# The context's tails on 128 partitions, the last key added by VectorE, five small loads moved one tile of tokens later

## The chip, the cores and the metric

The kernel runs on one core of a Trainium2 chip. The metric is the device time of one execution in microseconds (us). Before the change, three runs took 673.49, 671.36 and 673.45 us; the median is 673.45.

## The reference

A small Perceiver layer in float32, in three blocks with residual sums: cross-attention to a context, linear attention with an MLP, and a mixture of experts. Only the first block is touched. There are 8 sequences of 64 tokens with 512 features (`x`), and each sequence attends to a context of its own of 1601 keys:

```python
def _L0_xattn_ref(proj_p, proj_q, W, b):
    trans_q = jnp.einsum('bqh,oh->bqo', proj_q, W) + b
    att_weights = jnp.einsum('bph,bqh->bpq', proj_p, trans_q)
    att_norm = jax.nn.softmax(att_weights, axis=-1)
    att_vec = jnp.einsum('bpq,bqh->bph', att_norm, proj_q)
    out = jax.nn.relu(jnp.einsum('bph,oh->bpo', att_vec, W) + b)
    return out
...
x = x + _L0_xattn_ref(_layernorm(x, axis=-1), ctx_1024, L0_xattn_W, L0_xattn_b)
```

`proj_p` is the normalized `x` (8, 64, 512), `proj_q` the context (8, 1601, 512). The context is read twice: once transposed for the scores, once by rows for the weighted sum.

## The kernel before, in words

**Tiles.** The 512 tokens are four tiles of 128 (`NT` = 4). A tile holds two sequences, 64 tokens each, in the two halves of the 128 partitions. For a tile `t` the work is:

- `key_group(t, g)`, g = 0 to 3 (L412): the scores against 401 or 398 keys, from the transposed context (`ctxT`); for each half a product of 128 rows by 64 columns. ScalarE brings them into the buffer `scores` with the bias `pb` (L431). After the fourth group `softmax` (L437) takes the maximum on VectorE and the exponential on ScalarE, with the row sums.
- `turn_scores(t)` (L445): TensorE transposes the exponentials in blocks of 128 keys (L456), and ScalarE copies them into `eT` (L457). The 1601 keys are three groups of 512 and a tail of 65 (`TAIL`). The tail's block is one transpose to 65 partitions (L459) and one copy (L460).
- `weigh(t, g)`, g = 0 to 2 (L464): the weighted sum of the context's rows (`ctx`) in one PSUM bank `av`, for each half a product of 128 keys by 64 columns (L472). After the third group the tail's product is added (L482), with 65 keys in the contraction, and VectorE scales the sum by the inverse row sum into `av_sb` (L490).
- `turn_av(t)` (L492, the transposes at L495, VectorE's copy at L497), `attended(t)` (L499, the product with W at L502), `add_and_normalize(t)` (L506), `turn_h(t)` (L514) and `values(t, n)` (L528, the product at L532), which belongs to the linear attention that follows.

TensorE carries out a float32 product as two passes, so the profile counts two instructions for each product; a transpose is one.

**Order.** `tc.manual_schedule` makes every engine and SP's queue follow the order in which the program is written out. The loop over tiles (L541 to L569) interleaves the groups of one tile with the key groups of the next ones: behind the third `weigh` of tile `t` come `key_group(t + 2, 0)`, `turn_av(t)`, `key_group(t + 2, 1)` and `attended(t)`; for the last two tiles `values(t - 2, 0)` and `values(t - 2, 1)` take the place of the key groups.

**Loads.** All large loads come from SP's queue in the order of a list (L133 to L167). They go to a ring of 12 buffers, of up to 1 MB each; a load can be written out when the load 12 places earlier is done with (`issue_to`, L175). For tile `t` the list has rows 0, keys 2 of the next tile, rows 1, keys 3 of the next tile, rows 2, the tail, then keys 0 and 1 of tile `t + 2`; every rows or keys entry is two loads, one for each sequence. Behind tile 2's tail stand the two halves of `wv`, and behind tile 3's tail `wq`, `wk`, `wo` and the weights of the MLP. The tails have two buffers of their own (L74) and are loaded by one DMA each, to partitions 0 to 64, with both sequences side by side (L188).

**late_loads.** This function (L402) issues five DMAs from SP: it writes zeros, taken from the part of `v_sb` for tile 3, to the spare rows of the output and to the table of the experts' tokens, and loads the bias `b2_bc` and, in two halves, `proj2`. It is called once, behind the third `weigh` of tile 1 (L557). `proj2` is first used by the linear attention (L611).

Of the kernel before, what the change touches and what calls it, by code (L numbers as in the profile page):

```python
# [17 lines left out]
ALU = mybir.AluOpType  # L18
AX = mybir.AxisListType

P = 128
B, S, D = 8, 64, 512
LK = 1601
NT = B * S // P
KC = D // P
GK = 512
NG = LK // GK
TAIL = LK - NG * GK
SW = -(-LK // 4)
WIDTHS = [min(SW, LK - SW * g) for g in range(4)]  # L30
H, DH = 16, 64
# [15 lines left out]
def perceiver_kernel(  # L47
# [22 lines left out]
    nc = tc.nc  # L70
# [11 lines left out]
    def mm_bank(name):  # L82
        return ps.tile([P, 512], F32, tag="mm", name=name)

    def acc_bank(name):
        return ps.tile([P, 512], F32, tag="acc", name=name)
# [85 lines left out]
    def in_ring(key):  # L172
        return key[0] not in places_of and key not in places_of and key[0] != "tail"

    def issue_to(n):  # L175

        while issued[0] < min(n, len(order)):
            key, src = order[issued[0]]
            if in_ring(key) and len(held) >= RING:
                if held[0] not in freed:  # L180
                    return
                held.pop(0)
            if key in places_of:
                t_ = places_of[key]
                nc.sync.dma_start(t_, src)
            elif key[0] == "tail":
                t_ = tails.tile([P, 2, D], F32, tag="tail", name="_".join(str(k) for k in key))
                nc.sync.dma_start(t_[:TAIL, :, :], src)  # L188
            else:
                width = WIDTHS[key[2]] if key[0] == "ctxT" else 512  # L190
                t_ = ring.tile([P, 4, width], F32, tag="ring", name="_".join(str(k) for k in key))
                nc.sync.dma_start(t_, src)
                held.append(key)
            streamed[key] = t_
            issued[0] += 1

    def done(*keys):

        freed.update(keys)

    def need(*key):
        if key[0] not in ("ctxT", "ctx", "tail", "wv"):
            done(*[k for k in held if place[k] < place[key] - AHEAD + 1])
            issue_to(place[key] + 1 + AHEAD)
        else:
            issue_to(len(order))
        return streamed[key]


    ident = const.tile([P, P], F32, name="ident")  # L210
# [153 lines left out]
    def pw_half(half, hc):  # L364
# [10 lines left out]
        nc.scalar.copy(pw_t[:, hc, cols], bank[:, : 2 * P])  # L375

    issue_to(len(order))
    turn_p(0)
    turn_p(1)
# [22 lines left out]
    def late_loads():  # L402
        nc.sync.dma_start(out[B * S :, :], zero[:, :D])
        nc.sync.dma_start(table.rearrange("p k two -> p (k two)"), zero[:, : NE * NI * 2])
        nc.sync.dma_start(b2_bc, b2.partition_broadcast(P))
        for r in range(2):
            nc.sync.dma_start(proj2[r * DH : (r + 1) * DH, :], proj)


    all_scores, all_rinv, all_et = {}, {}, {}  # L410

    def key_group(t, g):  # L412

        if t >= NT:
            return
        if g == 0:
            all_scores[t] = xa2.tile([P, LK], F32, tag="scores", name=f"scores_{t}")
        width = WIDTHS[g]
        sc = acc_bank(f"sc_{t}_{g}")
        keys = [need("ctxT", t, g, h) for h in range(2)]  # L420
        for c in range(KC):
            for h in range(2):
                nc.tensor.matmul(  # L423
                    sc[h * S : (h + 1) * S, :width],
                    pw_t[:, c, (2 * t + h) * S : (2 * t + h + 1) * S],
                    keys[h][:, c, :],
                    start=(c == 0),
                    stop=(c == KC - 1),
                )
        done(*[("ctxT", t, g, h) for h in range(2)])  # L430
        nc.scalar.activation(  # L431
            all_scores[t][:, g * SW : g * SW + width], sc[:, :width], AF.Identity, bias=pb[:, t : t + 1]
        )
        if g == 3:
            softmax(t)
# [9 lines left out]
    def turn_scores(t):  # L445
        scores = all_scores[t]
        rinv = small.tile([P, 1], F32, tag="rinv", name=f"rinv_{t}")
        nc.vector.reciprocal(rinv, all_rinv[t])
        all_rinv[t] = rinv
        e_t = all_et[t] = xa.tile([P, 4 * NG + 1, P], F32, tag="w", name=f"eT_{t}")  # L450
        for g in range(NG + 1):
            bank = mm_bank(f"et_{t}_{g}")
            if g < NG:
                for j in range(4):
                    k = g * GK + j * P
                    nc.tensor.transpose(bank[:, j * P : (j + 1) * P], scores[:, k : k + P], ident)  # L456
                nc.scalar.copy(e_t[:, 4 * g : 4 * g + 4, :].rearrange("p j q -> p (j q)"), bank)  # L457
            else:
                nc.tensor.transpose(bank[:TAIL, :P], scores[:, NG * GK : LK], ident)  # L459
                nc.scalar.copy(e_t[:TAIL, 4 * NG, :], bank[:TAIL, :P])  # L460

    all_av, all_xo = {}, {}

    def weigh(t, g):  # L464

        if g == 0:
            all_av[t] = acc_bank(f"av_{t}")
        av, e_t = all_av[t], all_et[t]
        rows = [need("ctx", t, g, h) for h in range(2)]
        for j in range(4):  # L470
            for h in range(2):
                nc.tensor.matmul(  # L472
                    av[h * S : (h + 1) * S, :],
                    e_t[:, 4 * g + j, h * S : (h + 1) * S],
                    rows[h][:, j, :],
                    start=(g == 0 and j == 0),
                    stop=False,
                )
        done(*[("ctx", t, g, h) for h in range(2)])
        if g == NG - 1:  # L480
            for h in range(2):
                nc.tensor.matmul(  # L482
                    av[h * S : (h + 1) * S, :],
                    e_t[:TAIL, 4 * NG, h * S : (h + 1) * S],
                    need("tail", t)[:TAIL, h, :],
                    start=False,
                    stop=True,
                )
            av_sb = all_av[t] = xa2.tile([P, D], F32, tag="tmp", name=f"av_sb_{t}")
            nc.vector.tensor_scalar(av_sb, av, all_rinv[t], None, ALU.mult)  # L490

    def turn_av(t):  # L492
        bank = mm_bank(f"avt_{t}")
# [12 lines left out]
    def add_and_normalize(t):  # L506
        o_sb = xa2.tile([P, D], F32, tag="tmp", name=f"o_sb_{t}")
        nc.vector.tensor_tensor(o_sb, all_xo[t], xb_bc, ALU.add)
        nc.vector.scalar_tensor_tensor(xs[:, t, :], o_sb, 0.0, xs[:, t, :], ALU.max, ALU.add)
        normalize(xin[:, t, :], xs[:, t, :], *statistics(xs[:, t, :], f"xin_{t}"), f"xin_{t}")  # L510
        hns[t] = xa2.tile([P, D], F32, tag="tmp", name=f"hn_{t}")
        normalize(hns[t], xin[:, t, :], *statistics(xin[:, t, :], f"h_{t}"), f"h_{t}")

    def turn_h(t):  # L514
        bank = mm_bank(f"tr_h_{t}")
        for c in range(KC):
            nc.tensor.transpose(bank[:, c * P : (c + 1) * P], hns[t][:, c * P : (c + 1) * P], ident)
        for c in range(KC):
            nc.vector.tensor_scalar(  # L519
                h_t[:, c, t * P : (t + 1) * P],  # L520
                bank[:, c * P : (c + 1) * P],
                g1_c[:, c : c + 1],
                beta1_c[:, c : c + 1],
                ALU.mult,
                ALU.add,
            )

    def values(t, n):  # L528
        wv_n = need("wv", n)
        bank = mm_bank(f"v_{n}_{t}")  # L530
        for c in range(KC):
            nc.tensor.matmul(  # L532
                bank, h_t[:, c, t * P : (t + 1) * P], wv_n[:, c, :], start=(c == 0), stop=(c == KC - 1)
            )
        nc.scalar.copy(v_sb[:, t, n * 512 : (n + 1) * 512], bank)
# [5 lines left out]
    for t in range(NT):  # L541
        turn_scores(t)
        if t == NT - 1:

            nc.scalar.activation(warm0, eps, AF.Sqrt)
        if t > 0:
            add_and_normalize(t - 1)
        weigh(t, 0)
        key_group(t + 1, 2)
        if 0 < t < NT - 1:  # L550
            turn_h(t - 1)
        weigh(t, 1)
        if t == NT - 1:
            turn_h(t - 1)
        key_group(t + 1, 3)
        weigh(t, 2)
        if t == NT - 3:  # L557
            late_loads()

        if t < NT - 2:  # L560
            key_group(t + 2, 0)
        else:
            values(t - 2, 0)
        turn_av(t)
        if t < NT - 2:
            key_group(t + 2, 1)
        else:
            values(t - 2, 1)
        attended(t)  # L569
# [411 lines left out]
    bank = mm_bank("counts")  # L981
# [446 lines left out]
```

## Time and profile before

| What | Value |
|---|---|
| Median of three runs | 673.45 us (671.36 to 673.49) |
| The profiled execution | 672.11 us, of which the span in the trace is 670.4 us |
| Mean granted TensorE clock | 0.981 |
| PE busy | 627.2 us (94%) |
| DVE, ACT, POOL busy | 175.5, 128.3, 61.6 us |
| DMA | 138.08 MB, mean 206 GB/s |
| PE L472, the weighted sum | 50.2 us busy, 7.3 us idle before it |
| PE L482, the tail's product | 6.8 us busy in 16 instructions |
| SP L188, the tail's load | 4 DMAs of 260 KB |

PE is TensorE's matmuls, PEld its weight loads, DVE is VectorE, ACT is ScalarE, POOL is GpSimd, SP is SyncE, whose queue (SPq) issues the loads. In the page's second part the span is cut into 40 equal slices, and each digit is a share in tenths. A line of the timeline has start, duration, engine, line of the kernel, operation, the tile written and the tiles read, and in brackets the idle time ahead and what ended it. A line of the windows has the busy time of each engine with its number of instructions, then the granted clock, the DMA engines' share and the GB/s moved. A group of instructions has the shapes, the number, the busy time, the mean duration in ns, and the idle time ahead of it.

### The profile page before, as it was taken

Reading aid. Unit: us, or ns where it says so; the run is one execution under the profiler, and the core shown is the slowest. Engines: PE = TensorE matmul, PEld = TensorE weight load, DVE = VectorE, ACT = ScalarE, POOL = GpSimd, SP = SyncE. Lnnn points to the kernel's source line nnn. Section 1 sums busy time; section 2 is a strip of 40 time slices with the busy share of each in tenths; the row PEclk is TensorE's granted clock in tenths of the full one; section 3 lists DMA queues with packets and bytes.
Section 4 is the critical chain, followed back from the end, with each engine's and each line's share of the span. In section 5 each row is a group of like instructions: output and inputs, shape, how many; then the busy total and the mean of one; then the engine's idle time right before and its main releaser. Section 6 shows DMA issues by size and latency. Waiting matters only on the chain. (4 is left out here: it accounts for less than half of the span.)

```text
span 670.4 us, 6808 instructions
## 1 busy us (share of the span) xinstructions
PE 627.2 (94%) x2664; PEld 291.2 (43%) x2664; DVE 175.5 (26%) x419; ACT 128.3 (19%) x240; POOL 61.6 (9%) x81
## 2 busy tenths in 40 slices
PE   4998989799999999999999998899999899999993
PEld 3743434243444444454444455433444344334441
DVE  4011323122316888650000045311210111100100
ACT  2241222220132223031011211211111211111110
POOL 2000000000000000060000001340202202210000
PEclk9998999899999999999999999799999999999997
DMA  8999999999421203030213115029389576694611
GB/s 326 420 420 389 420 384 418 374 386 413 194 111 43 85 1 127 1 126 18 107 64 125 63 64 188 3 69 350 137 314 337 176 314 229 205 359 177 269 16 19
DMA packets 24224, 138.08 MB, mean 206 GB/s; under 512 B 4164, under 2 KB 4164, under 8 KB 11896
## 3 DMA queue, kind: packets, MB, share of 16 engines
q1 hardware_dynamic: 20056, 129.90, 49.7%
q0 software_dynamic: 3024, 6.58, 4.4%
q10 hardware_dynamic: 1104, 1.07, 0.5%
q8 instruction: 25, 0.41, 0.2%
q14 instruction: 15, 0.12, 0.1%
HBM read 132.56 MB, written 4.97 MB: 205 GB/s over the span
## 5 line engine op out<-in xcount | busy, mean ns | idle before, releaser
L1097 PE MATMUL up<-e_up,xgT 128*128 128x512 f32 x224 | 100.2, 595 | 1.2 <-PEq L1326 1.2
L1097 PEld LDWEIGHTS up<-e_up,xgT 128*128 128x128 f32 x224 | 40.9, 190 | 50.4 <-issue 50.4
L1105 PE MATMUL y<-e_wo,hidT 128*128 128x512 f32 x128 | 61.0, 599 | 0.0
L808 PE MATMUL mlp<-w,hid_sb 128*128 128x512 f32 x128 | 58.8, 597 | 0.0
L1062 DVE TENSOR_TENSOR mid<-up,act 128x256 f32<-128x256 f32 x35 | 14.9, 425 | 162.4 <-ACT act L1060 162.4
L472 PE MATMUL av<-ctx,eT 128*64 128x512 f32 x192 | 50.2, 636 | 7.3 <-DMA ctx<-in_ctx_dram 6.5
L787 PE MATMUL hid<-v_sb,w 128*128 128x512 f32 (+2 forms) x144 | 56.6, 545 | 0.0
L423 PE MATMUL sc<-ctxT,pw_t 128*64 128x401 f32 (+1 forms) x256 | 48.1, 501 | 0.6 <-DMA ctxT<-in_ctx_T_dram 0.6
L787 PEld LDWEIGHTS hid<-v_sb,w 128*128 128x128 f32 x144 | 26.2, 190 | 29.1 <-issue 27.3
L808 PEld LDWEIGHTS mlp<-w,hid_sb 128*128 128x128 f32 x128 | 23.4, 190 | 24.9 <-issue 24.9
L1060 ACT ACTIVATE act<-up 128x256 f32<-128x256 f32 x35 | 13.4, 384 | 104.5 <-PE up L1097 95.6
L1078 POOL DMA_INDIRECT out_dram<-y_sb,dst_late x11 | 16.8, 1530 | 160.9 <-ACTq L1326 103.7
L423 PEld LDWEIGHTS sc<-ctxT,pw_t 128*64 128x64 f32 x256 | 20.2, 136 | 26.0 <-issue 22.6
L802 POOL TENSOR_TENSOR xin<-xin,b_bc 128x512 f32<-128x512 f32 x4 | 5.1, 1269 | 283.4 <-DVE rstd_h L744 279.1
L1105 PEld LDWEIGHTS y<-e_wo,hidT 128*128 128x128 f32 x128 | 22.4, 190 | 19.5 <-issue 19.1
L472 PEld LDWEIGHTS av<-ctx,eT 128*64 128x64 f32 x192 | 15.2, 143 | 35.8 <-issue 24.3
L706 PE MATMUL wo<-wo,a_t 128*128 128x512 f32 x64 | 29.1, 600 | 0.5 <-DVE a_t L682 0.5
L595 PE MATMUL wk<-h_t,wk 128*128 128x512 f32 x64 | 29.5, 604 | 0.0
L595 PE MATMUL wq<-h_t,wq 128*128 128x512 f32 x64 | 29.4, 602 | 0.0
L532 PE MATMUL v<-wv,h_t 128*128 128x512 f32 x64 | 28.7, 597 | 0.6 <-DVE h_t L519 0.6
L680 DVE RECIPROCAL rden<-rden 128x512 f32<-128x512 f32 x8 | 26.8, 3353 | 0.3
L844 DVE TENSOR_TENSOR xs<-mlp,xs 128x512 f32<-128x512 f32 x4 | 2.8, 691 | 87.3 <-PE mlp L808 87.3
(229 smaller groups left out, 630.0 us busy)
## 6 DMA issues: line engine op xcount, KB each, us to landing
e_up<-in_L_ffn_up_dram SPq DMA_DIRECT2D x32, 1024.0 KB, 7.8
ctx<-in_ctx_dram SPq DMA_DIRECT2D x24, 1024.0 KB, 17.4
ctxT<-in_ctx_T_dram SPq DMA_DIRECT2D x24, 802.0 KB, 15.7
e_wo<-in_L_ffn_wo_dram SPq DMA_DIRECT2D x16, 1024.0 KB, 11.3
w<-in_L_attn_w_dram SPq DMA_DIRECT2D x8, 1024.0 KB, 10.9
ctxT<-in_ctx_T_dram SPq DMA_DIRECT2D x8, 796.0 KB, 16.7
big_up<-in_L_ffn_up_dram SPq DMA_DIRECT2D x4, 1024.0 KB, 7.9
wv<-in_L_attn_wv_dram SPq DMA_DIRECT2D x2, 1024.0 KB, 13.1
```

Source lines behind the costliest of these rows:

```text
L423: nc.tensor.matmul(sc[h * S : (h + 1) * S, :width], pw_t[:, c, (2 * t + h) * S : (2 * t + h + 1) * S], keys[h][:, c, :], start=(c == 0), s ...
L472: nc.tensor.matmul(av[h * S : (h + 1) * S, :], e_t[:, 4 * g + j, h * S : (h + 1) * S], rows[h][:, j, :], start=(g == 0 and j == 0), stop=F ...
L532: nc.tensor.matmul(bank, h_t[:, c, t * P : (t + 1) * P], wv_n[:, c, :], start=(c == 0), stop=(c == KC - 1))
L595: nc.tensor.matmul(bank, w[:, c, (j % 4) * P : (j % 4 + 1) * P], h_t[:, c, :], start=(c == 0), stop=(c == KC - 1),)
L680: nc.vector.reciprocal(rden, rden)
L706: nc.tensor.matmul(wo_banks[t], a_t[:, j, t * P : (t + 1) * P], wo_r[j // 4][:, j % 4, :], start=(j == 0), stop=(j == nj - 1),)
L787: nc.tensor.matmul(hid_banks[f][:, tokens], w[:, c, (f % 4) * P : (f % 4 + 1) * P], h2_t[:, c, tokens], start=(c == 0), stop=(c == KC - 1),)
L808: nc.tensor.matmul(acc[t], hid[:, t * P : (t + 1) * P], need("w2", f // 4)[:, f % 4, :], start=(f == 0), stop=(f == FF // P - 1),)
L1062: nc.vector.tensor_tensor(hid, bank[:, FQ:], act, ALU.mult)
L1078: nc.gpsimd.indirect_dma_start(out=out, out_offset=bass.IndirectOffsetOnAxis(ap=dst[:n, :], axis=0), in_=y_sb[:n, :], in_offset=None, boun ...
L1097: nc.tensor.matmul(bank, xg_t[:, c, :], up_of[q][:, c, :], start=(c == 0), stop=(c == KC - 1))
L1105: nc.tensor.matmul(y, h_t[:, j, :], w[:, 2 * (q % 2) + j, :], start=(q + j == 0), stop=(q + j == NQ))
```

## The change

The tail becomes 64 keys for each sequence (`TAIL` = 64), and the last key, number 1601, is handled apart.

- The tail's source is laid out anew: for each tile 128 rows of 4 KB. Row p has in its first half the tail key p modulo 64 of the sequence p // 64, and in its second half the last key's features of that sequence, repeated for all 64 rows. The load fills all 128 partitions and grows from 260 to 512 KB.
- `turn_scores` replaces the tail's transpose by two products with the identity, one for each half, from the partitions of a half to the same partitions. ScalarE copies 128 partitions by 64 columns.
- The tail's product in `weigh` has 64 keys in the contraction, with both operands of a sequence in its half of the partitions and its result in the same half.
- VectorE adds the last key: its features times the exponential in the last column of `scores`, plus `av`, into `av_sb`. The scaling by the inverse row sum follows as an operation of its own on `av_sb`.
- `late_loads` is called behind the third `weigh` of tile 2 instead of tile 1.

```diff
-TAIL = LK - NG * GK
+TAIL = LK - NG * GK - 1
...
-                nc.sync.dma_start(t_[:TAIL, :, :], src)
+                nc.sync.dma_start(t_, src)
...
-                nc.tensor.transpose(bank[:TAIL, :P], scores[:, NG * GK : LK], ident)
-                nc.scalar.copy(e_t[:TAIL, 4 * NG, :], bank[:TAIL, :P])
+
+                for h in range(2):
+                    part = slice(h * S, (h + 1) * S)
+                    nc.tensor.matmul(
+                        bank[part, :S],
+                        scores[part, NG * GK : NG * GK + TAIL],
+                        ident[part, part],
+                        start=True,
+                        stop=True,
+                    )
+                nc.scalar.copy(e_t[:, 4 * NG, :S], bank[:, :S])
...
-                    e_t[:TAIL, 4 * NG, h * S : (h + 1) * S],
-                    need("tail", t)[:TAIL, h, :],
+                    e_t[h * S : (h + 1) * S, 4 * NG, :S],
+                    need("tail", t)[h * S : (h + 1) * S, 0, :],
...
-            nc.vector.tensor_scalar(av_sb, av, all_rinv[t], None, ALU.mult)
+
+            nc.vector.scalar_tensor_tensor(
+                av_sb, need("tail", t)[:, 1, :], all_scores[t][:, LK - 1 : LK], av, ALU.mult, ALU.add
+            )
+            nc.vector.tensor_scalar(av_sb, av_sb, all_rinv[t], None, ALU.mult)
...
-        if t == NT - 3:
+        if t == NT - 2:
             late_loads()
...
-    inputs["ctx_tail"] = tail.reshape(NT, 2, TAIL, D).transpose(0, 2, 1, 3)
+    last = _np.broadcast_to(tail[:, TAIL:, :], (B, TAIL, D))
+    inputs["ctx_tail"] = _np.stack([tail[:, :TAIL, :], last], axis=2).reshape(NT, P, 2, D)
```

## The prediction

> **What bounds the kernel now.** I read the page first for where the change lies in time. It touches only the cross-attention, and every tail and every moved load falls before 160 us of the 670.4 us span.
>
> ```profile
> PEclk9998999899999999999999999799999999999997
> DMA  8999999999421203030213115029389576694611
> ```
>
> One digit is 16.8 us. In the first ten slices the DMA engines are full, and TensorE's granted clock dips in slices 4 and 8. So in this stage arrivals set the pace; from slice 11 on the DMA is mostly idle. The waits of the stretch 0 to 200 us give 6.5 us for PE L472 on ctx and 9.1 us for its weight loads. Next the timeline of PE shows where:
>
> ```profile
> 58.09 1.04 PE L472 MATMUL av<-ctx,eT 128*64 128x512 f32 x2
> 61.51 4.92 PE L472 MATMUL av<-ctx,eT 128*64 128x512 f32 x13 [2.38 <-DMA ctx<-in_ctx_dram]
> ...
> 94.34 3.22 PE L472 MATMUL av<-ctx,eT 128*64 128x512 f32 x13 [1.45 <-DMA ctx<-in_ctx_dram]
> ...
> 128.98 4.92 PE L472 MATMUL av<-ctx,eT 128*64 128x512 f32 x13 [2.65 <-DMA ctx<-in_ctx_dram]
> ...
> 135.11 3.70 PE L532 MATMUL v<-wv,h_t 128*128 128x512 f32 x8
> ```
>
> Each wait is in the third row group of a tile of tokens, for the second sequence's rows: the load directly ahead of the tail in SP's queue. No DMA wait follows 128.98, so what counts is when that wait ends and how fast TensorE runs just after it. The windows by 3 us show what the DMA does there (clock, DMA share, GB/s are the last three):
>
> ```profile
> 55.00:58.00 3.00, 3.00 (x17) 1.04 (x14) 0.00 (x0) 0.00 (x0) 0.00 (x0) 1.00 0.99 411
> 58.00:61.00 3.00, 1.13 (x4) 0.19 (x2) 1.82 (x1) 0.68 (x2) 0.00 (x0) 1.00 1.02 270
> 61.00:64.00 3.00, 2.49 (x8) 0.78 (x10) 0.00 (x0) 1.64 (x2) 0.00 (x0) 0.63 1.00 395
> ...
> 91.00:94.00 3.00, 1.89 (x10) 0.42 (x5) 1.26 (x1) 1.88 (x2) 0.00 (x0) 1.00 1.01 255
> ...
> 127.00:130.00 3.00, 1.02 (x6) 0.45 (x8) 0.00 (x0) 1.72 (x2) 0.00 (x0) 1.00 0.99 306
> 130.00:133.00 3.00, 3.00 (x10) 0.77 (x8) 0.00 (x0) 0.00 (x0) 0.00 (x0) 0.51 1.02 423
> ```
>
> The engines stay "full", but move 255 to 306 GB/s instead of 420. These dips are the tails: in the trace's packets the 65 packets of 4 KB of each tail start just there, with medians of 218 to 261 ns, where the 4 KB packets of xs took 159 ns; packets of other loads beside them go from 245 to about 460 ns. After the long waits of tiles 0 and 2 the clock is granted at 0.63 and 0.51.
>
> [...]
>
> **The change part by part.** Prices of instructions are from the groups kept apart by shape, and SP's queue from its timeline:
>
> ```profile
> L482 PE MATMUL av<-tail,eT 65*64 65x512 f32 x16 | 6.8, 602 | 0.0
> L490 DVE TENSOR_SCALAR av_sb<-av,rinv 128x512 f32<-128x512 f32 x4 | 3.0, 751 | 22.5 <-PE av L482 22.5
> L626 DVE SCALAR_TENSOR_TENSOR phi_wq<-pr_wq,ex_wq 128x512 f32<-128x512 f32 x1 | 0.7, 692 | 0.2 <-ACT ex_wq L623 0.2
> L346 DVE TENSOR_SCALAR xin<-xs,mv_xin,rstd_xin 128x512 f32<-128x512 f32 x4 | 2.2, 546 | 0.1
> ```
>
> ```profile
> 101.44 2.28 SPq L192 DMA_DIRECT2D ctxT<-in_ctx_T_dram  x2
> 105.89 0.34 SPq L403 DMA_DIRECT2D out_dram<-v_sb  x1
> ...
> 112.24 2.96 SPq L407 DMA_DIRECT2D proj<-in_L_attn_proj_dram  x2
> 117.26 2.26 SPq L192 DMA_DIRECT2D ctx<-in_ctx_dram  x2
> ```
>
> *The tail load.* It grows from 260 to 512 KB: at 420 GB/s 0.63 becomes 1.25 us, +0.62. What it loses is the dip. Landings (issue plus time to landing in the DMA view) around tail 0: rows at 57.95, first keys after it at 64.54, 6.59 us for 1024 + 260 + 802 KB = 2.136 MB, which need 5.09 at 420. Dip 1.50. Around tail 1: 90.78 to 99.41, 8.63 us for 2.957 MB, 7.04 needed, dip 1.59. So each tail hands later loads 1.50 - 0.62 = 0.88 and 1.59 - 0.62 = 0.97 us. A 128-row load without a dip is what xs shows; bounds: no dip at all, or a dip that grows with the bytes (rival C).
>
> *The rows ahead of it.* For tile 2 the first rows land at 125.15 and the second are there at 128.93: 3.78 us for 1 MB that takes 2.50 at 420 GB/s. [...] Without a dip, -1.28.
>
> *late_loads.* Five DMAs, 576 KB, stand ahead of tile 2's third rows. From the last keys but one (119.13) to 125.15 are 6.02 us; 796 + 1024 KB alone need 4.44. So -1.58 before these rows. After the change they follow tile 2's third group: by then the ring has let SP issue wv, the rows and tail of tile 3, and all wq and wk (142.95 now). They pass those on SP's queue and stand ahead of wo and w only; POOL's queue isn't touched. SP lets about eight DMAs be out at a time, so each issue waits for an older landing, some 2 us: wo comes up to 11 us later, and is used far later (first at 261 us). proj is first used at 195.76; v_sb's last part, which two of them read, is overwritten after 178; landing by about 160, both have over 15 us. Without that cover ACT's copy would wait the excess.
>
> *The wait of tile 2.* 0.88 + 0.97 + 1.58 + 1.28 = 4.71: it ends at 124.27 instead of 128.98. TensorE must be ready: its key block ends at 121.62 + 2.85 = 124.47 now, and it starts from the keys that ended its wait at 99.41, which come 1.85 earlier; so about 122.7, half a microsecond for the first rows, and a wait of 1.1. Even with infinitely early rows only that 1.1 is left to win.
>
> *The clock.* From 128.98 to 135.11 the 18 instructions left take 6.13 us; at 0.219 each (16 in 3.5 at full clock) 3.94. A wait of 1.1 us, [...] should save 2.19.
>
> *TensorE's own work.* The tail's four passes (0.88 us a tile) become 64*64 on the diagonal. L611 starts four such within 20 ns and takes 0.43 to 0.48 for the four; [...] I take 0.58, -0.3. One transpose becomes four short matmuls; 32 of L637 take 0.62 us, [...] +0.1. ACT's copy shrinks from 128 to 64 columns, off the path.
>
> *VectorE.* 0.692 + 0.546 replace 0.751: +0.49 a tile, before turn_av. It is covered by the block of keys (2.9) or values (3.6): at tile 0 av_sb is ready at 68.55 and L495 starts at 70.35. Uncovered it would cost 0.49 each. New waits: the added operation waits for tail and av; behind it stand the scaling and avT. ACT's next write of that scores buffer now waits for it, but comes only after 2.9 us of key matmuls. The tail's buffer is freed 0.7 us later; its next load is over 30 us away.
>
> *Sum.* Resume 124.27 + 3.94 - 0.3 = 127.9; wv's first half lands 124.22 + 1.25 + 2.50 = 128.0, so values start at 128.0 instead of 135.11: -7.1. Tile 3 adds -0.3 + 0.1. Together -7.3; its loads land earlier by more, so no new DMA wait. After 180 us the weights' issues wait for TensorE, so the gain goes through. The profiled execution took 672.11 (span 670.4, 1.7 around it), 1.34 below the median 673.45: 664.8 for it, 666.2 for the median.
>
> **Rivals.** *A, the clock still drops* at tile 2[...]: 2.2 comes back, 668.4. [...] *B, absorbed*: late_loads hold wo and w back by up to 11 us, and if a weight's landing had less than that to spare, a wait of up to 7.3 would take the gain: about 673. Against: wo lands at 168 now and is used 93 us later, and SP's later issues wait on PE. *C, slower*: the dip comes not of 65 rows but of the tail's own source or 4 KB pieces, and doubles with the bytes. Then tails 0 and 1 cost 0.62 + 1.5 more each, tile 2's rows another 1.28, less 1.58: +3.9, 677.4. It decides from a dip of about 2.6 us in place of 1.5. Against it: xs's 4 KB packets at 159 ns. [...]
>
> **How the numbers follow.** Main 0.64, A 0.18, B 0.08, C 0.10. Range: low end, main with 1.1 from even earlier rows, 0.4 more on the tail passes[...], 663.0; high end, A with half of the dips left (2.2), 670.6. Faster by over 0.3% is main, A and a part of B: 0.85; within 0.3%, about what a measurement of this kernel can tell from no change, 0.06; slower 0.09.
>
> **What would show it.** Right: windows around the tails at about 415 GB/s; no 2.4 us waits at L472; clock 1.00 from 124 to 134; late loads after wk in SP's timeline; values at about 128. Wrong: dips that stay, the same clock loss, L495 or L431 waiting for VectorE, or 64*64 tail passes at 0.43 each.

## The result and the profile after

The changed kernel takes 666.76 us (median of 6 runs, 666.01 to 667.88), the kernel before 673.26 us in the same runs; the ratio is 0.9909, with a 95% interval of 0.9893 to 0.9924. It is faster by 6.5 us. The profiled execution took 667.88 us, with a span of 666.1, and is the longest of the six.

The timeline of PE after, at the three waits of before and behind the last one (lines move by 9 to 13: the rows' product is L481 now, the tail's L491, the values' L545):

```profile
60.53 3.65 PE L481 MATMUL av<-ctx,eT 128*64 128x512 f32 x14 [1.36 <-DMA ctx<-in_ctx_dram]
64.11 1.08 PE L491 MATMUL av<-tail,eT 64*64 64x512 f32 x4
...
92.52 3.65 PE L481 MATMUL av<-ctx,eT 128*64 128x512 f32 x14 [0.77 <-DMA ctx<-in_ctx_dram]
...
124.32 3.65 PE L481 MATMUL av<-ctx,eT 128*64 128x512 f32 x14 [0.61 <-DMA ctx<-in_ctx_dram]
127.90 1.08 PE L491 MATMUL av<-tail,eT 64*64 64x512 f32 x4
128.90 3.70 PE L545 MATMUL v<-wv,h_t 128*128 128x512 f32 x8
```

The waits of 2.38, 1.45 and 2.65 us are 1.36, 0.77 and 0.61, and the last one ends at 124.32 instead of 128.98. The values start at 128.90 instead of 135.11. The windows after (the last three columns are clock, DMA share and GB/s):

```profile
58.00:61.00 3.00, 1.64 (x6) 0.39 (x6) 1.82 (x1) 0.62 (x2) 0.00 (x0) 1.00 1.04 423
61.00:64.00 3.00, 3.00 (x14) 0.85 (x10) 0.00 (x0) 1.70 (x2) 0.00 (x0) 1.00 1.01 415
...
91.00:94.00 3.00, 2.23 (x10) 0.63 (x10) 1.82 (x1) 2.40 (x3) 0.00 (x0) 1.00 1.04 424
...
124.00:127.00 3.00, 2.68 (x13) 0.96 (x14) 1.38 (x1) 2.41 (x3) 0.00 (x0) 1.00 1.01 421
...
130.00:133.00 3.00, 3.00 (x12) 1.52 (x11) 0.29 (x1) 0.36 (x1) 0.00 (x0) 1.00 1.00 415
```

The dips are gone: 423 GB/s in place of 270, 424 in place of 255, 421 in place of 306, and the clock is never granted below 1.00 here. In the trace's packets, the tails' 4 KB pieces take 159 to 161 ns in the median; before it was 218 to 261. SP's timeline shows late_loads in their new place, behind wk and ahead of wo:

```profile
138.04 0.33 SPq L192 DMA_DIRECT2D wk<-in_L_attn_wk_dram  x1
140.53 0.34 SPq L403 DMA_DIRECT2D out_dram<-v_sb  x1
...
146.73 2.97 SPq L407 DMA_DIRECT2D proj<-in_L_attn_proj_dram  x2
151.76 2.81 SPq L192 DMA_DIRECT2D wo<-in_L_attn_wo_dram  x2
```

A good mark for the end of the touched stretch is the first product with wq, before and after:

```profile
185.36 3.60 PE L595 MATMUL wq<-h_t,wq 128*128 128x512 f32 x8
```

```profile
179.45 3.60 PE L608 MATMUL wq<-h_t,wq 128*128 128x512 f32 x8
```

It starts 5.91 us earlier. Up to the router (the part of the third block that assigns tokens to experts) the distance stays at 5.91 (its first transposes start at 415.41 and 409.50). Then the clock takes some of it back in this execution. Two windows around the idle time of the router, of before and of after:

```profile
416.00:430.00 14.00, 11.31 (x34) 7.74 (x34) 5.87 (x46) 3.37 (x5) 4.18 (x5) 0.63 0.18 60
```

```profile
410.00:425.00 15.00, 12.24 (x34) 7.82 (x33) 5.96 (x47) 2.80 (x5) 4.91 (x5) 0.54 0.18 57
```

Before, 14 x 0.37 = 5.2 us are lost to the clock, after 15 x 0.46 = 6.9: 1.7 us more. Behind this stretch the distance is 4.44 us (products that start at 432.42 and 427.98). Nothing of the change lies here. The six runs of after fall in two groups, 666.0 to 666.3 with a mean clock of 0.986 or 0.987 and 667.3 to 667.9 with 0.985, and the profiled one belongs to the second.

### The profile page after: what moved, and what is told of

The parts are those of the page before. It is cut to its first block, busy times and chain, and to the rows that moved or that the text cites. A ratio compares the mean times of both kernels' runs of the same rounds, so it can differ in the third digit from the quotient of the medians.

```text
span 666.1 us, 6844 instructions
## 1 busy us (share of the span) xinstructions
PE 627.9 (94%) x2676; PEld 292.1 (44%) x2676; DVE 177.4 (27%) x423; ACT 128.1 (19%) x240; POOL 61.5 (9%) x81
## 5 line engine op out<-in xcount | busy, mean ns | idle before, releaser
L481 PE MATMUL av<-ctx,eT 128*64 128x512 f32 x192 | 46.7, 598 | 2.7 <-DMA ctx<-in_ctx_dram 2.7
L545 PE MATMUL v<-wv,h_t 128*128 128x512 f32 x64 | 28.7, 597 | 0.6 <-DVE h_t L532 0.6
L481 PEld LDWEIGHTS av<-ctx,eT 128*64 128x64 f32 x192 | 13.7, 136 | 28.7 <-issue 22.9
```

The costliest lines, as they stand in the source:

```text
L481: nc.tensor.matmul(av[h * S : (h + 1) * S, :], e_t[:, 4 * g + j, h * S : (h + 1) * S], rows[h][:, j, :], start=(g == 0 and j == 0), stop=F ...
L545: nc.tensor.matmul(bank, h_t[:, c, t * P : (t + 1) * P], wv_n[:, c, :], start=(c == 0), stop=(c == KC - 1))
```

## The experiments

My theory was that the load of 65 rows slows all DMA traffic around it, and that late_loads ahead of tile 2's rows are a second, smaller cost. The rivals were that late_loads are the whole gain, that the new products are part of it, and that the dip belongs to the tensor or its bytes. The first four kernels take the change apart.

**Only late_loads moved.**

```diff
-        if t == NT - 3:
+        if t == NT - 2:
             late_loads()
```

> The kernel before with only the call of late_loads moved to tile 2. My theory (the 65-row tail load is the main cost, late_loads the smaller one): the five loads' 1.6 us leave the queue ahead of tile 2's third rows, so its wait ends at about 127.4 instead of 128.98; the dips of 255 to 306 GB/s at the tails stay; the idle stretch is still near 2.9 us, so the clock may still fall. About 671.7 us, 670 if the clock stays up. Rival (late_loads are the whole gain): about 667.

Measured: 670.6 us, ratio 0.996 (0.994 to 0.998). The timeline of PE:

```profile
127.36 4.91 PE L472 MATMUL av<-ctx,eT 128*64 128x512 f32 x13 [2.31 <-DMA ctx<-in_ctx_dram]
...
133.50 3.70 PE L532 MATMUL v<-wv,h_t 128*128 128x512 f32 x8
```

Its windows:

```profile
91.00:94.00 3.00, 1.14 (x4) 0.14 (x1) 1.82 (x1) 2.04 (x3) 0.00 (x0) 1.00 1.00 270
127.00:130.00 3.00, 2.64 (x10) 0.94 (x12) 0.00 (x0) 1.48 (x2) 0.00 (x0) 0.79 1.00 384
```

The wait ends 1.62 us earlier and the whole stage 1.61 (wq at 183.75). The dip stays (270 GB/s), and so does the clock's loss: after the wait, 6.14 us pass up to the values, as the 6.13 of before. late_loads are not the whole gain.

**Only the tail changed**, late_loads at tile 1 as before; the edit is one of the changed kernel.

```diff
-        if t == NT - 2:
+        if t == NT - 3:
             late_loads()
```

> The changed kernel with late_loads back at tile 1. My theory: the tails run at about 415 GB/s without a dip, but the five loads stand again ahead of tile 2's third rows and add 1.6 us: the wait ends at about 125.9. About 668.4 us if the clock stays up after an idle stretch of 2.3 us, 670.1 if it falls to half for one window. Rival (late_loads are the whole gain): about 673.

Measured: 669.25 us, ratio 0.9944 (0.9927 to 0.9960). The wait of tile 2 ends at 126.35, 2.03 us later than with both parts, and wq starts at 181.48. The clock stays up: behind a wait of 1.37 us the 14 passes of the rows take 3.65 us, as in the changed kernel. So the tail alone gives 3.88 of the 5.91 us, and late_loads bring the other 2.03 in these two executions.

**Only the load padded.** Products, transpose and VectorE are those of before; the tail's source gets rows of zeros, and the load fills 128 partitions.

```diff
-                nc.sync.dma_start(t_[:TAIL, :, :], src)
+                nc.sync.dma_start(t_, src)
...
-    inputs["ctx_tail"] = tail.reshape(NT, 2, TAIL, D).transpose(0, 2, 1, 3)
+    padded = _np.zeros((NT, P, 2, D), _np.float32)
+    padded[:, :TAIL] = tail.reshape(NT, 2, TAIL, D).transpose(0, 2, 1, 3)
+    inputs["ctx_tail"] = padded
```

> The kernel before with its 65-row contraction, transpose and single VectorE operation kept, and only the tail's source padded with 63 rows of zeros, so that the load fills 128 partitions (512 KB). late_loads stay at tile 1. My theory (the shape of the load is what counts, not the form of the products): no dips, wait of tile 2 ends at about 125.9, and TensorE saves the 0.2 to 0.3 us a tile that the 64*64 products cost; about 668 us, 669.6 if the clock falls. Rival (a dip comes with this tensor or with its bytes): dips twice as long, about 677. Rival (the gain comes from the new products): about 674.

Measured: 668.49 us, ratio 0.9927 (0.9904 to 0.9949).

```profile
180.69 3.60 PE L595 MATMUL wq<-h_t,wq 128*128 128x512 f32 x8
```

wq starts 4.67 us earlier than before, from one line of the load and its source, while the load's bytes double. The rival of the tensor or its bytes falls, and so does that of the new products: with the old ones wq starts 0.79 us earlier than in the kernel with only the tail changed. Of this, 0.36 is an earlier end of tile 2's wait (125.99 against 126.35), though the loads have the same sizes and order: that much such a wait differs between single executions.

**The load padded and late_loads moved.** Both edits together on the kernel before.

> The kernel before with the tail padded to 128 rows and late_loads at tile 2, products and VectorE as before. My theory: all of the change's gain, and 0.2 us at tile 2 and 0.3 us at tile 3 more[...]: about 666.3 us, the tail's four passes overlapping the rows' again. Rival (the new products carry part of the gain): about 668 to 670.

Measured: 666.87 us, ratio 0.9909 (0.9885 to 0.9933).

```profile
179.03 3.60 PE L595 MATMUL wq<-h_t,wq 128*128 128x512 f32 x8
```

wq starts 0.42 us earlier than with the change, while the wait of tile 2 ends at the same time (124.33). In whole times it can't be told from the changed kernel: the padding and the move give the whole gain.

The next four ask what is wrong with 65 rows, and the last one whether VectorE's added work is covered. The three kernels with rows in parts were run once each, beside a median of 672.18 us of the kernel before, so only what their traces show is taken from them.

**64 rows and one**, on the kernel before.

```diff
-                nc.sync.dma_start(t_[:TAIL, :, :], src)
+                nc.sync.dma_start(t_[: TAIL - 1, :, :], src[: TAIL - 1])
+                nc.sync.dma_start(t_[TAIL - 1 : TAIL, :, :], src[TAIL - 1 :])
```

> The kernel before, each tail loaded by two DMAs: 64 rows and the last row alone. It tells two forms of my theory apart. If the number of rows is what hurts[...], the dips at the tails vanish or shrink to the single row: windows there at 400 GB/s or more, about 669 us. If it is that the rows lie in partitions 0 to 64 only[...], the dips stay at 255 to 310 GB/s: about 673 us.

Measured: 675.93 us. **Two halves of 64 partitions**, on the changed kernel:

```diff
-                nc.sync.dma_start(t_, src)
+                for h in range(2):
+                    nc.sync.dma_start(t_[h * S : (h + 1) * S, :, :], src[h * S : (h + 1) * S])
```

> The changed kernel, each tail loaded by two DMAs of 64 rows, partitions 0 to 63 and 64 to 127, same bytes. [...] If filling only half of the partitions by one DMA hurts, each half dips (255 to 310 GB/s), twice as long as before: rows of tile 2 come 3 us or more later, 671 us or more.

Measured: 681.5 us. **104 rows and 24**, on the changed kernel:

```diff
-                nc.sync.dma_start(t_, src)
+                nc.sync.dma_start(t_[:104, :, :], src[:104])
+                nc.sync.dma_start(t_[104:, :, :], src[104:])
```

> The changed kernel, each tail loaded by two DMAs of 104 and 24 rows, same bytes, all partitions filled. [...] If the spread over partitions is what counts, [...] dips clearly smaller than 255 to 306 GB/s, about 668 us.

Measured: 676.24 us. **Cut by columns**, the control of the halves: two DMAs of the same size, each over all 128 partitions.

```diff
-                nc.sync.dma_start(t_, src)
+                for h in range(2):
+                    nc.sync.dma_start(t_[:, h, :], src[:, h, :])
```

> The changed kernel, each tail loaded by two DMAs of 256 KB that both fill all 128 partitions, cut along the columns (2 KB a row). It is the control of the cut into two halves of partitions. If the halves were slow because each DMA filled only part of the partitions: no dips here, at least 400 GB/s at the tails, 667 us within 0.3%. If they were slow because there were two smaller DMAs: dips as with the halves, 675 us or more.

Measured: 666.88 us, ratio 0.9905 (0.9888 to 0.9921). The same two windows at tile 0's tail, first of the halves, then of the cut by columns, then of 104 and 24 rows:

```profile
58.00:61.00 3.00, 1.11 (x4) 0.19 (x2) 1.82 (x1) 0.70 (x2) 0.00 (x0) 1.00 1.07 221
61.00:64.00 3.00, 0.87 (x2) 0.29 (x4) 0.00 (x0) 1.62 (x2) 0.00 (x0) 0.68 1.00 250
```

```profile
58.00:61.00 3.00, 1.64 (x8) 0.44 (x8) 1.82 (x1) 0.70 (x2) 0.00 (x0) 1.00 1.03 404
61.00:64.00 3.00, 3.00 (x14) 0.80 (x10) 0.00 (x0) 1.61 (x2) 0.00 (x0) 1.00 1.03 423
```

```profile
58.00:61.00 3.00, 1.39 (x6) 0.27 (x2) 1.76 (x1) 0.59 (x1) 0.00 (x0) 1.00 1.09 226
61.00:64.00 3.00, 1.28 (x6) 0.48 (x8) 0.06 (x1) 1.72 (x2) 0.00 (x0) 0.90 0.97 257
```

The DMA share is about 1.0 in all of them; only the GB/s tell them apart. Same bytes and, in the first two, the same number of DMAs of 256 KB: 221 and 250 GB/s against 404 and 423. So neither size nor number of DMAs makes the dip. In the shapes tried, what goes with it is that a DMA fills only a part of the partitions. The odd 65th row is not needed for it: the halves of 64 rows dip too, and in the kernel with 64 rows and one the window 58 to 61 moves 202 GB/s. That all rows of a load lie on half of the partitions does not explain it either: with 104 and 24 rows the window moves 226 GB/s, and the smaller dips that go with that reading did not come. Which property of a partial load slows the others stays open: no trace here tells which DMA engine carried a packet, and for the tail no other partial loads than those of 1, 24, 64, 65 and 104 rows were measured.

**More work on VectorE**, on the changed kernel:

```diff
             nc.vector.tensor_scalar(av_sb, av_sb, all_rinv[t], None, ALU.mult)
+            for _ in range(2):
+                nc.vector.tensor_scalar(av_sb, av_sb, 1.0, None, ALU.mult)
```

> The changed kernel with two more VectorE operations on av_sb (times 1.0) behind the scaling, 0.97 us a tile. My theory (VectorE's added work is covered by the key or value products that stand ahead of turn_av, with about 2.1 us to spare): no change, 666.8 us within 0.3%. Rival (the chain through VectorE is on the path): 1 us a tile, up to 670.7 us.

Measured: 667.14 us, ratio 0.9921 (0.9901 to 0.9942). The two operations took 0.89 us a tile, a little less than the 0.97 expected, and wq starts at 179.47, against 179.45. The timeline of VectorE at tile 0:

```profile
65.25 0.75 DVE L500 SCALAR_TENSOR_TENSOR av_sb<-tail,scores,av 128x512 f32<-128x512 f32 x1 [4.29 <-PE av L491]
66.03 0.49 DVE L503 TENSOR_SCALAR av_sb<-av_sb,rinv 128x512 f32<-128x512 f32 x1
66.56 0.89 DVE L505 TENSOR_SCALAR av_sb<-av_sb 128x512 f32<-128x512 f32 x2
69.29 0.69 DVE L512 COPY avT<-avt 128x512 f32<-128x512 f32 x1 [1.85 <-PE avt L510]
```

Even with them VectorE stands idle for 1.85 us before it is needed again. The chain through VectorE is off the path.

## Why the prediction was right, step by step

**The tail load: right in direction and size.** The dips vanished. The rows of tile 2 land at 121.78 and 124.28, 2.50 us apart as forecast, instead of 3.78. For the end of tile 2's wait the three terms of the tail came to 0.88 + 0.97 + 1.28 = 3.13 us; the tail alone moved it by 2.63 (128.98 to 126.35), the padding alone by 2.99 (to 125.99). That the shape of the load does it is shown by the padded kernel and by the control pair. All five shapes tried agree: 128 rows run at 404 GB/s and more, and 65, 64 + 1, 64 + 64 and 104 + 24 dip to between 202 and 319. The packets of the traces show it too: in the window 124 to 130 the 8 KB packets of the rows take 402 ns in the median before, 313 after. Why a partial load slows the packets beside it was not shown.

**late_loads: right.** Forecast 1.58 us; 1.62 alone, 1.66 on top of the padding (the wait ends at 125.99 and 124.33), 2.03 on top of the tail. The 0.4 between 1.62 and 2.03 is about what the end of such a wait differs by between single executions (0.36 above). With the padding the two parts add up: 1.61 + 4.67 = 6.28 us up to wq, against 6.33 measured together. One cost did not come: wo, for which up to 11 us of delay were allowed, landed at 160.68 and 163.17, some 5 us earlier than before (165.74 and 168.22). The eight DMAs that SP lets be out can be read in both traces: an issue comes just behind the landing of the load eight places ahead, after at 121.84 and 124.34 behind landings at 121.78 and 124.28, before at 46.55 behind one at 46.49.

**The end of the wait: right.** Forecast 124.27, measured 124.32.

**The clock: right in kind, its term too large.** No loss is left, as forecast. But the 2.19 us taken as its price compared 6.13 with 18 x 0.219 = 3.94. The traces have ten slots of 0.43 us or a little more in this stretch: a column half that waits for its rows shifts the two halves against each other, and its last passes run alone (after at 126.95 and 127.37). The kernel with the padded load and late_loads moved has the same instructions at full clock and takes 4.44 us for them (124.33 to 128.77). The clock's part is 6.13 - 4.44 = 1.69, which the windows of before give too (3 x 0.49 + 3 x 0.08 = 1.7). The waits ahead of the two losses were 2.38 and 2.65 us; the one of 1.45 us at tile 1 left the clock at 1.00 (windows 91 to 97), and after, behind 0.61 us at tile 2, it is 1.00 too.

**TensorE's own work: wrong in sign.** Forecast -0.3 for each tail and +0.1 for the short products. The 0.58 us for the tail was the author's estimate; after, its four instructions take 1.00 us from the first start to the values (127.90 to 128.90). The step failed in what it took 0.219 us for: it read this as the time of one pass, while the passes of the two column halves start 6 to 8 ns apart and a pair takes 0.43. Before the change the tail's passes (L482 has 16 instructions for eight products, two for each) already shared their slots, at tile 3 with each other (158.56 to 159.52 for the four) and at tile 2 with the rows, so the diagonal form gains nothing. It costs: before, the first of the tail's passes run beside the rows' last ones, as the timeline of before shows, where rows and tail alternate.

```profile
133.16 0.74 PE L482 MATMUL av<-tail,eT 65*64 65x512 f32 x1
133.73 0.59 PE L472 MATMUL av<-ctx,eT 128*64 128x512 f32 x1
133.74 1.45 PE L482 MATMUL av<-tail,eT 65*64 65x512 f32 x3
```

After, L491 starts 0.52 us behind the last pass of L481 (127.37 to 127.90), which has its slot to itself; slots of passes of one shape are 0.43 apart. From the wait's end to the values it takes 4.58 us, 0.14 more than the form of before at full clock, and not the 3.64 forecast; of the 0.94 between, 0.50 are the clock's term and 0.44 the tail's. At tile 3, where nothing waits for a load, the stretch from the values to wq grew from 50.25 to 50.55 us, against a forecast of -0.2. About half of the 0.3 are the short products: from the first transpose to the first rows it takes 1.66 us (139.75 to 141.41) in place of 1.51.

**VectorE: right.** 0.747 + 0.487 in place of 0.751, covered.

**The sum.** 7.3 forecast for the stage, 5.91 measured: the clock, the tail of tile 2 and tile 3 make 0.50 + 0.44 + 0.50 = 1.44, all of the difference of 1.39. That the time itself came within 0.6 us of the forecast is in part luck: the medians differ by 6.5 us, the means of the same runs by 6.2, the two profiled executions by 4.2. The two groups of runs after lie 1.4 us apart in the mean, and the median falls between them. Why the medians gain 0.6 more than the stage no trace here settles.

## What to carry to other kernels

Where DMA sets the pace, look for stretches in which the engines' share stays full and the GB/s fall, and ask which load begins there; here one small load over part of the partitions brought the total from about 420 to between 255 and 306 GB/s, and padding it to 128 rows with zeros was worth 4.7 us though its bytes doubled. Loads that nothing needs soon belong behind those that set the pace; here that was worth 1.6 to 2.0 us. Before a product is recast to use less of the array, check by start times whether its parts already run side by side, as they did here, 6 to 8 ns apart.

## What the runs showed that I had not expected

- DMAs of 64 partitions did no better than one of 65: with the 512 KB load cut into two halves of partitions the windows at tile 0 moved 221 and 250 GB/s, and the one run took 681.5 us, with the clock at 0.68 in the window 61 to 64, while cutting it by columns cost nothing that shows in the median (666.88; wq at 179.84).
- Two 128*64 products with their results in different column halves run side by side in the traces before and after: starts 6 to 8 ns apart, 0.43 us for a pair of passes over 512 columns. A pair of 64*64 products on the diagonal takes no less, 0.48 from its start to the next pair's, and some 0.1 us more passes at the change from the one shape to the other (0.52 in place of 0.43).
- Waits of 1.36, 1.37 and 1.45 us in this stage left TensorE's clock alone (after at tile 0, the tail alone at tile 2, before at tile 1), and those of 2.31, 2.38 and 2.65 us each went with a loss (windows of 0.79 with only late_loads moved, 0.63 and 0.51 before). In the trace's record of the granted clock it is 0.50 before for 3.41 us from 61.77, 3.41 us from 130.04 and 10.24 us from 416.76; these starts are 20 and 84 times 3.41 us apart. After, it is 0.50 for 13.65 us from 410.32 and again from 659.49, 73 such steps later. So the 1.7 us at the router are one step more at half clock, 13.65 us in place of 10.24. Counted from the start of the span, the steps of the two executions lie 0.39 us apart.
